# Routed expert outputs scattered to token rows, with GpSimd weighing half of them at the end of a decoder layer

## The chip, the cores and the metric

The kernel runs on one core of a Trainium2 chip. Five engines with queues of their own work on one on-chip memory: TensorE (PE, matrix products into the accumulator memory PSUM), VectorE (DVE), ScalarE (ACT), GpSimd (POOL) and SyncE (SP, which mostly issues DMAs). [...]The metric is device time in microseconds, a median over runs; the profile is one execution recorded by the hardware.

## What is computed

One post-norm decoder layer on 2048 tokens of 256 features (8 sequences of 256), in float32: self-attention with 16 heads, then three rounds of slot attention with a gated recurrent cell against a context of 120 rows, then a feed-forward stage, each followed by a layer norm. The change touches only the last stage:

```python
router_probs = softmax(x @ gate_w + gate_b)                   # 8 experts
expert_values, expert_indices = top_k(router_probs, k=2)
expert_values = expert_values / (sum(expert_values) + 1e-09)
h = gelu(einsum('bsd,edi->bsei', x, ew1) + eb1)
all_outputs = einsum('bsei,eid->bsed', h, ew2) + eb2
moe_out = einsum('bse,bsed->bsd', weights_E, all_outputs)      # the chosen two only
return layernorm(2 * x + mlp(x, sh_w1, sh_b1, sh_w2, sh_b2) + moe_out)
```

(The layer norm gets the residual sum once more, so x enters twice.) Each token needs two of the eight experts and, besides, one shared MLP with the same sizes (256 to 1024 to 256).

## The kernel before

Tokens lie in four blocks of 512 (`X[i]`, 128 partitions by 4 groups of 128 tokens by 256 features); `XT[i]` is the same block transposed, `Z[i]` the block's output sum.

**Routing.** When a block leaves the second stage, `route_rest` finds its two experts (`hot1`, `hot2`, weights `wt1`, `wt2`). `place(i)` gives each of the 1024 (token, choice) pairs a row in a table `xd` in DRAM, in which every expert owns 2048 rows, and scatters the tokens there: eight indirect DMAs from GpSimd's queue, 128 rows of 1 KB each (L909). Rows without a token stay zero, for which both `xd` and `yd` were filled with zeros earlier (L543), each 16640 rows.

**Tiles.** `tables` (L920) cuts the rows in use into 23 tiles, 16 of 256 rows and 7 of 128, each of one expert, whose number and first row are read from SBUF into registers of SyncE (`value_load`, L1130 and L1144). Per tile, `tile_fetch` loads its rows (`xg`), `tile_weights` and `tile_weights2` load the expert's two 1 MB matrices, `tile_turn` transposes the rows on TensorE and copies them out on VectorE (`xgT`), `tile_up` does the first product with GELU on ScalarE, `tile_down` the second, adds the bias on VectorE (`yo`), and stores it to the same rows of `yd` (L1180).

**Shared MLP.** It runs in eight units of 256 tokens: `shared_up(u)` and two halves of `shared_down(u)`. Units 0 to `SHARED_FIRST` - 1 = 3 stand before the tiles and cover the routing; units 4 to 7 stand after them.

**The end.** `fetch_back(i)` gathers the two outputs of each token from `yd` by the slots that `place` had computed (eight indirect DMAs of 128 rows on GpSimd's queue per block, L1190). `take_back(i)` adds them, weighted, to `Z[i]` in eight VectorE instructions (L1204). `finish` is the layer norm: statistics on VectorE (L221, L222), reciprocal root by Ln and Exp on ScalarE (L130, L131), three small refining steps (L236 to L238) and the scaling (L242) on VectorE, then the store.

**What sets the order.** TensorE and ScalarE follow the program everywhere. VectorE and GpSimd are ordered by a planner during the middle of the kernel, but from the last `tile_down` on all four follow the order in which the program is written. SyncE's queue is ordered by the planner. A DMA on SyncE's queue also waits for the DMA eight before it on the same semaphore.

Of the kernel before, what the change touches and what calls it, by code (L numbers as in the profile page):

```python
# [10 lines left out]
F32 = mybir.dt.float32  # L11
I32 = mybir.dt.int32
# [32 lines left out]

ROWS = NE * NT + RT

SHARED_FIRST = 4

NY = 16  # L50
LN_EPS = 1e-5
RMS_EPS = 1e-6
ATT_EPS = 1e-6
# [8 lines left out]
def decoder_kernel(  # L62
# [44 lines left out]
            nc.scalar.copy(dst, src)  # L107


    X = [act.tile([P, NSUB, D], F32, tag=f"X{i}", name=f"X{i}") for i in range(NBLK)]  # L110
    XT = [act.tile([P, DC, BLK], F32, tag=f"XT{i}", name=f"XT{i}") for i in range(NBLK)]

    def load_x(i):
# [36 lines left out]
    )  # L150


    xd = tc.dram_tile([ROWS, D], F32, name="xd")
    yd = tc.dram_tile([ROWS, D], F32, name="yd")


    for h in range(2):
# [378 lines left out]
    b2p = stage2.enter_context(tc.tile_pool(name="b2", bufs=2))  # L536

    shared = load_shared()
    zeros = b1.tile([P, D], F32, name="zeros")
    nc.gpsimd.memset(zeros, 0.0)  # L540

    for table in (xd, yd):
        nc.sync.dma_start(  # L543
            table.rearrange("(p r) d -> p r d", p=P), zeros.unsqueeze(1).to_broadcast([P, ROWS // P, D])
        )

    fh = ctx.enter_context(tc.tile_pool(name="fh", bufs=2, side="right"))

# [1 line left out]
    nsub_all = NBLK * NSUB  # L550
    hot1 = fr.tile([P, nsub_all, NE], F32, name="hot1")
    hot2 = fr.tile([P, nsub_all, NE], F32, name="hot2")
    wt1 = fr.tile([P, nsub_all], F32, name="wt1")
    wt2 = fr.tile([P, nsub_all], F32, name="wt2")
    slots = [fr.tile([P, nsub_all], I32, name=f"slot{j}") for j in range(2)]

    cur = fr.tile([P, nsub_all, NE], F32, name="cur")
# [272 lines left out]
    def route_rest(i):  # L830

        shape = [P, NSUB, NE]

        def t(name):
            return fr2.tile(shape, F32, tag=name, name=f"{name}_{i}")

        def s(name):
            return fr2.tile([P, NSUB], F32, tag=name, name=f"{name}_{i}")

        def wide(a):  # L840
            return a.unsqueeze(2).to_broadcast(shape)

        pl = bank(f"pl_{i}")[:, 0 : NSUB * NE].rearrange("p (n e) -> p n e", e=NE)
        for n in range(NSUB):
            for dc in range(DC):
                nc.tensor.matmul(
                    pl[:, n, :], XT[i][:, dc, ts(n, P)], gate_sb[:, dc, :], start=dc == 0, stop=dc == DC - 1
                )
        pb, mx, sm = t("pb"), s("mx"), s("sm")
        tt(pb, pl, gate_b.unsqueeze(1).to_broadcast(shape), ALU.add)  # L850
        nc.vector.tensor_reduce(mx, pb, AX.X, ALU.max)
        tt(pb, pb, wide(mx), ALU.subtract)
        nc.scalar.activation(pb, pb, AF.Exp)
        nc.vector.tensor_reduce(sm, pb, AX.X, ALU.add)
        nc.vector.reciprocal(sm, sm)
        tt(pb, pb, wide(sm), ALU.mult)
        rankb = rank.unsqueeze(1).to_broadcast(shape)

        def best(src, k, hot):
            top, first = s(f"top{k}"), s(f"first{k}")  # L860
            nc.vector.tensor_reduce(top, src, AX.X, ALU.max)
            tt(hot, src, wide(top), ALU.is_equal)
            tt(hot, hot, rankb, ALU.mult)
            nc.vector.tensor_reduce(first, hot, AX.X, ALU.max)
            tt(hot, hot, wide(first), ALU.is_equal)
            return top

        blk = ts(i, NSUB)
        top1 = best(pb, 1, hot1[:, blk, :])
        rest = t("rest")  # L870
        nc.vector.scalar_tensor_tensor(rest, hot1[:, blk, :], -2.0, pb, ALU.mult, ALU.add)
        top2 = best(rest, 2, hot2[:, blk, :])
        den = s("den")
        tt(den, top1, top2, ALU.add)
        nc.vector.tensor_scalar(den, den, TOPK_EPS, None, ALU.add)
        nc.vector.reciprocal(den, den)
        tt(wt1[:, blk], top1, den, ALU.mult)
        tt(wt2[:, blk], top2, den, ALU.mult)
        tt(cur[:, blk, :], hot1[:, blk, :], hot2[:, blk, :], ALU.add)
        for g in range(i * NSUB, (i + 1) * NSUB):  # L880
            tt(before[:, g + 1, :], before[:, g, :], cur[:, g, :], ALU.add)


    puts = []

    def place(i):

# [18 lines left out]
        for n in range(NSUB):  # L906
            for slot in slots:
                g = i * NSUB + n
                put = nc.gpsimd.indirect_dma_start(  # L909
                    out=xd[:, :],  # L910
                    out_offset=bass.IndirectOffsetOnAxis(ap=slot[:, g : g + 1], axis=0),
                    in_=X[i][:, n, :],
                    in_offset=None,
                )
                if puts:
                    tc.declare_no_dep(put.ins, group="puts", reason="other rows")
                tc.add_to_no_dep_group("puts", put.ins)
                puts.append(put)

    def tables():  # L920

# [77 lines left out]
        for a, b, n in ((te, te2, float(NE)), (tr, tr2, none)):  # L999
            nc.vector.scalar_tensor_tensor(b, b, -n, free, ALU.add, ALU.mult)  # L1000
            tt(a, a, b, ALU.add)
        nc.vector.tensor_scalar(te, te, float(NE - 1), None, ALU.min)
        tei = fr.tile([P, NTILE], I32, name="tei")
        nc.vector.tensor_copy(tei, te)
        tri = fr.tile([P, NTILE], I32, name="tri")
# [111 lines left out]
        tt(z, z, po, ALU.add)  # L1117
        yield

    TI = {}  # L1120

    def groups(t):
        return 2 if t < NPAIRT else 1
# [4 lines left out]
    def tile_fetch(t):  # L1128

        row = nc.sync.value_load(tri[0:1, t : t + 1], min_val=0, max_val=ROWS - RT)  # L1130
        xg = f2.tile([P, 2, D], F32, tag="xg", name=f"xg_{t}", bufs=4)[:, 0 : groups(t), :]
        load = nc.sync.dma_start(xg, rows_of(xd, row, t))
        for put in puts:
            tc.add_manual_dep(
                load.ins,
                put.ins.name,
                mybir.DependencyInfo(mybir.DependencyClass.Sync, mybir.DependencyReason.DATA),
                reason="rows of the table",
            )
        TI[t] = [row, xg]  # L1140

    def tile_weights(t):

# [4 lines left out]
        b2t = f2.tile([P, D], F32, tag="b2t", name=f"b2t_{t}", bufs=3)  # L1148
        nc.sync.dma_start(w1_sb, ew1[ds(e, 1), :, :].rearrange("e (c p) f -> p (e c) f", p=P))
        nc.sync.dma_start(bt, vecs[:, ds(e * FC, FC)])  # L1150
        TI[t] += [w1_sb, w2_sb, bt, b2t, e]

    def tile_weights2(t):

        row, xgT, w1_sb, w2_sb, bt, b2t, e = TI[t]
        nc.sync.dma_start(w2_sb, ew2[ds(e, 1), :, :].rearrange("e (c p) d -> p (e c) d", p=P))
        nc.sync.dma_start(b2t, b2[ds(e, 1), :].to_broadcast([P, D]))

    def tile_turn(t):
# [5 lines left out]
                nc.tensor.transpose(pt[:, dc, ts(k, P)], xg[:, k, ts(dc, P)], ident)  # L1165
        xgT = f2.tile([P, DC, RT], F32, tag="xgT", name=f"xgT_{t}")[:, :, 0 : n * P]
        nc.vector.tensor_copy(xgT, pt)  # L1167
        TI[t][1] = xgT

    def tile_up(t):  # L1170
        row, xgT, w1_sb, w2_sb, bt, b2t, e = TI[t]
        HT["t", t] = up(w1_sb, bt, xgT, f"t{t}")

    def tile_down(t):
        row, xgT, w1_sb, w2_sb, bt, b2t, e = TI.pop(t)
        n = groups(t)
        po = down(w2_sb, HT.pop(("t", t)), f"t{t}", groups=n)
        yo = f2.tile([P, 2, D], F32, tag="yo", name=f"yo_{t}")[:, 0:n, :]
        tt(yo, po[:, 0:n, :], b2t.unsqueeze(1).to_broadcast([P, n, D]), ALU.add)
        nc.sync.dma_start(rows_of(yd, row, t), yo)  # L1180

    Y = {}

    def fetch_back(i):

        for n in range(NSUB):
            for j, slot in enumerate(slots):
                g = i * NSUB + n
                y = f2.tile([P, D], F32, tag="y", name=f"y_{g}_{j}", bufs=NY)
                nc.gpsimd.indirect_dma_start(  # L1190
                    out=y,
                    out_offset=None,
                    in_=yd[:, :],
                    in_offset=bass.IndirectOffsetOnAxis(ap=slot[:, g : g + 1], axis=0),
                )
                Y[g, j] = y

    def take_back(i):

        for n in range(NSUB):  # L1200
            g = i * NSUB + n
            for j, wt in enumerate((wt1, wt2)):
                z = Z[i][:, n, :]
                nc.vector.scalar_tensor_tensor(z, Y.pop((g, j)), wt[:, g : g + 1], z, ALU.mult, ALU.add)  # L1204

    def finish(i, n0, n1):
        layernorm(Z[i][:, n0:n1, :])
# [11 lines left out]
    def parts(u):  # L1219
        next(part[u])  # L1220
        next(part[u])
# [11 lines left out]
    place(3)  # L1233
    next(part[1])
    tei, tri = tables()
    for t in TILES[:2]:
        tile_fetch(t)
    tile_weights(TILES[0])
    tile_weights2(TILES[0])
    for u in range(2, SHARED_FIRST):  # L1240
        shared_up(u)
        if u == SHARED_FIRST - 1:
            tile_fetch(TILES[2])
            tile_weights(TILES[1])
            tile_turn(TILES[0])
        parts(u)
    for u in range(SHARED_FIRST, nunit):
        shared_bias(u)
    for k, t in enumerate(TILES):
# [14 lines left out]
    engines = {mybir.EngineType.PE, mybir.EngineType.Activation, mybir.EngineType.DVE, mybir.EngineType.Pool}  # L1264
    ctx.enter_context(tc.manual_schedule(engines=engines))
    half = NSUB // 2
    shared_up(4)
    fetch_back(0)
    shared_up(5)
    fetch_back(1)  # L1270
    take_back(0)
    parts(4)
    take_back(1)
    shared_up(6)
    nc.scalar.preload_act_table_set(LNEXP)
    for i in range(2):
        finish(i, 0, NSUB)
    fetch_back(2)
    parts(5)
    shared_up(7)  # L1280
    nc.scalar.preload_act_table_set(LNEXP)  # L1281
    take_back(2)
    finish(2, 0, NSUB)
    fetch_back(3)
    next(part[6])
    take_back(3)
    next(part[6])
    finish(3, 0, half)
    po = [bank(f"pf_s7_{a}")[:, 0:D] for a in range(half)]
    hT = HT.pop(("s", 7))  # L1290
# [71 lines left out]
```

## Time and profile before

| | before |
|---|---|
| median of 3 runs | 1041.12 us (1041.05 to 1042.68) |
| the profiled execution | 1039.3 us |
| its span | 1037.6 us |
| TensorE busy | 1023.9 us (99%), at a granted clock of 0.999 |
| VectorE busy | 486.6 us (47%), 1378 instructions |
| ScalarE busy | 466.3 us (45%) |
| GpSimd busy | 264.1 us (25%), 280 instructions |
| zero fill of xd and of yd | 16640 KB each, landed 51.3 us and 99.4 us after their issue |
| indirect DMAs to xd (L909) and from yd (L1190) | 32 and 32, 8.39 MB in all |
| DMA traffic | 144.24 MB, 139 GB/s on average |

The span is the time between the first and the last recorded event; 1.7 us of the execution lie outside it. A group in the profile is named by source line, engine and operation, with what it writes and reads; a time in square brackets is idle time of the engine before an instruction and what ended it. TensorE's busy time counts pipelined products, so 99% says that it hardly ever waits, not that each product is as fast as can be.

### The profile page before, as it was taken

To read this page: it belongs to the slowest core of one execution; us is meant where nothing else is said; L and a number is where in the kernel's file an instruction comes from. 1 tells how busy PE (TensorE), PEld (TensorE's weight loads), DVE (VectorE), ACT (ScalarE), POOL (GpSimd) and SP (SyncE) were. 2 spreads that over 40 slices of the span, in tenths; PEclk is the share of its full clock that TensorE was granted. 3 is DMA by queue.
4 is the path that set the end of the run, shared out by engine and by line. 5 is a ranking of instruction groups with operands and counts; after the bars stand their busy time and mean duration, and the time that the engine had idled before them with its cause. 6 is when DMAs were issued, how large, how long until landed. Compare 5 with 4: busy or idle time off the path is not lost. (4 is left out here: it accounts for less than half of the span.)

```text
span 1037.6 us, 13707 instructions
## 1 busy us (share of the span) xinstructions
PE 1023.9 (99%) x4686; PEld 711.2 (69%) x4686; DVE 486.6 (47%) x1378; ACT 466.3 (45%) x1156; POOL 264.1 (25%) x280
## 2 busy tenths in 40 slices
PE   9999999999999999999999999999999999999997
PEld 5444555555546755556565567988888888888886
DVE  4778776877897542444444579600010101010157
ACT  3568776766685034455455434322222322222232
POOL 2333422633587221122212014410000000000172
PEclk9999999999999999999999999999999999999999
DMA  9844434434467399950000001166666676765143
GB/s 324 132 76 93 86 69 76 77 62 76 77 115 161 125 348 348 349 172 0 1 1 0 1 16 57 62 193 228 219 219 213 224 235 221 230 208 194 50 121 103
DMA packets 195492, 144.24 MB, mean 139 GB/s; under 512 B 107551, under 2 KB 185951, under 8 KB 195423
## 3 DMA queue, kind: packets, MB, share of 16 engines
q1 hardware_dynamic: 191263, 132.88, 45.5%
q0 software_dynamic: 3072, 8.39, 2.5%
q10 hardware_dynamic: 1088, 2.10, 0.5%
q8 instruction: 37, 0.61, 0.2%
q14 instruction: 32, 0.26, 0.1%
HBM read 72.70 MB, written 45.48 MB: 114 GB/s over the span
## 5 line engine op out<-in xcount | busy, mean ns | idle before, releaser
L1071 ACT ACTIVATE hT_t<-ph_t,bt 128x256 f32<-128x256 f32 (+1 forms) x184 | 71.3, 438 | 202.6 <-issue 139.1
L353 ACT ACTIVATE sc<-sc,nmax 128x128 f32<-128x128 f32 (+1 forms) x256 | 113.2, 443 | 86.0 <-DVE nmax L340 85.5
L368 POOL TENSOR_TENSOR sc<-sc,sums 128x256 f32<-128x256 f32 (+1 forms) x128 | 105.4, 845 | 162.8 <-DVE sums L365 162.0
L1062 PE MATMUL ph_t<-xgT,w 128*128 128x256 f32 (+1 forms) x736 | 140.3, 348 | 0.8 <-ACT hT_t L1071 0.8
L1076 PE MATMUL pf_t<-w,hT_t 128*128 128x256 f32 x624 | 138.3, 379 | 0.0
L1062 PEld LDWEIGHTS ph_t<-xgT,w 128*128 128x128 f32 x736 | 123.8, 190 | 15.0 <-ACT hT_t L1071 1.0
L756 PE MATMUL gate<-XT,whh_sb 128*128 128x512 f32 x288 | 133.8, 593 | 0.0
L1076 PEld LDWEIGHTS pf_t<-w,hT_t 128*128 128x128 f32 x624 | 116.9, 190 | 15.0
L1190 POOL DMA_INDIRECT y<-yd,slot x32 | 31.0, 969 | 308.2 <-PE ph_s L1062 298.7
L396 DVE COPY pT<-turned 128x1536 uint16<-128x1536 uint16 x64 | 89.8, 1403 | 1.2 <-DMA turned<-planes 1.2
L756 PEld LDWEIGHTS gate<-XT,whh_sb 128*128 128x128 f32 x288 | 54.2, 189 | 48.5 <-issue 46.2
L340 DVE CUSTOM_DVE_ANT_0 sc<-pp,mask 128x128 f32<-128x128 f32 (+1 forms) x256 | 75.8, 352 | 8.8 <-PE pp L328 8.2
L1167 DVE COPY xgT<-xg 128x512 f32<-128x512 f32 (+1 forms) x23 | 14.0, 610 | 131.7 <-PE xg L1165 131.7
L765 PEld LDWEIGHTS gate<-at,G 120*128 120x128 f32 x288 | 54.5, 189 | 29.9 <-issue 23.3
L613 DVE TENSOR_TENSOR yo<-pf_t,b2t 128x512 f32<-128x512 f32 (+1 forms) x23 | 14.0, 610 | 127.9 <-PE pf_t L1076 127.9
L384 ACT COPY planes<-sc 128x1536 uint16<-128x1536 uint16 x48 | 70.6, 1470 | 6.7 <-POOL sc L368 6.7
L765 PE MATMUL gate<-at,G 120*128 120x256 f32 x288 | 72.1, 379 | 0.4 <-DVE at L613 0.4
L303 PE MATMUL pq<-XT,wq_sb 128*128 128x512 f32 x128 | 63.4, 618 | 0.2 <-DVE XT L105 0.2
L303 PE MATMUL pq<-XT,wk_sb 128*128 128x512 f32 x128 | 63.2, 616 | 0.0
L313 PE MATMUL pv<-wv_sb,XT 128*128 128x512 f32 x128 | 59.7, 594 | 0.0
L410 PE MATMUL po<-pT,v 128*64 128x256 f32 (+1 forms) x512 | 55.7, 338 | 2.4 <-DVE pT L396 1.5
L426 PE MATMUL py<-wo_sb,ot 128*128 128x256 f32 x256 | 57.9, 381 | 0.0
(209 smaller groups left out, 1429.5 us busy)
## 6 DMA issues: line engine op xcount, KB each, us to landing
w<-in_ew_dram SPq DMA_DIRECT2D x46, 1024.0 KB, 5.5
xd<-zeros SPq DMA_DIRECT2D x1, 16640.0 KB, 51.3
yd<-zeros SPq DMA_DIRECT2D x1, 16640.0 KB, 99.4
xg<-xd SPq DMA_DIRECT2D x16, 256.0 KB, 5.2
yd<-yo SPq DMA_DIRECT2D x16, 256.0 KB, 5.6
b2t<-in_b_dram SPq DMA_DIRECT2D x23, 128.0 KB, 5.3
sh<-in_sh_w_dram SPq DMA_DIRECT2D x2, 1024.0 KB, 6.6
X<-in_x_dram SPq DMA_DIRECT2D x3, 512.0 KB, 11.6
```

Of the source, the lines that this page charges most:

```text
L303: nc.tensor.matmul(pq, w[:, dc, ts(pr, P)], XT[i][:, dc, :], start=dc == 0, stop=dc == DC - 1)
L313: nc.tensor.matmul(pv, XT[i][:, dc, ts(n, P)], wv_sb[:, dc, ts(hf, 512)], start=dc == 0, stop=dc == DC - 1)
L340: nc.vector.tensor_tensor_reduce(out=sc[:, h, seg[t]], in0=pp[h][:, seg[t]], in1=mask[:, seg[t]], scale=-(HD**-0.5), scalar=3.0e38, op0=AL ...
L353: nc.scalar.activation(sc[:, h, seg[t]], sc[:, h, seg[t]], AF.Exp, scale=-1.0, bias=nmax[:, t, h : h + 1], accum_out=sums[:, t, h : h + 1],)
L368: nc.gpsimd.tensor_tensor(sc[:, :, seg[t]], sc[:, :, seg[t]], sums[:, t, :].unsqueeze(2).to_broadcast([P, 2, w]), ALU.mult,)
L384: nc.scalar.copy(planes, words)
L396: nc.vector.tensor_copy(pT.rearrange("p h c -> p (h c)").bitcast(U16).rearrange("p (n w) -> p w n", w=2), turned.rearrange("p (w c) q -> p ...
L756: nc.tensor.matmul(pg[:, oc, :], whh_sb[:, dc, o], XT[i][:, dc, :], start=dc == 0, stop=not given and dc == DC - 1,)
L765: nc.tensor.matmul(pg[:, oc, ts(bi, S)], G[:, BPB * i + bi, o], AT_[p][:, bi, :], start=not hidden, stop=not hidden or bi == BPB - 1,)
L1062: nc.tensor.matmul(ph[:, a, 0:w], w1_sb[:, dc, ts(c, P)], rhs[:, dc, :], start=dc == 0, stop=dc == DC - 1,)
L1071: nc.scalar.activation(hT[:, c, 0:w], ph[:, a, 0:w], AF.Gelu_apprx_tanh, bias=bias[:, c : c + 1])
L1076: nc.tensor.matmul(po, hT[:, c, ts(a, P)], w2_sb[:, c, :], start=c == 0, stop=c == FC - 1)
```

## The change

- **Token rows carry their address.** `X[i]` becomes the first 256 columns of `XW[i]`, 272 columns wide. Column 256 holds 2 x (token + 1), column 257 the rank of the token's first expert, which `best` now writes there. The rows of `xd` are 272 wide too (1088 bytes).
- **Scatter instead of gather.** In `tile_turn`, three small VectorE instructions per tile work out the target row of each output: 2 x (token + 1), plus one if the tile's expert is the token's first choice, or an unused row where the table row was empty. `tile_down` writes its rows there with one indirect DMA per 128 rows on GpSimd's queue (39 in all) in place of the plain store on SyncE's. `yd` has 9090 rows and is no longer filled with zeros. `fetch_back` becomes one plain load of 1 MB per block on SyncE's queue, which waits for all 39 scatters; it lands in the expert weights' buffers, and all four are issued at once.
- **Token scatters in pairs.** In `place`, a small GpSimd memset stands after each pair of scatters. It writes a spare column of the groups just sent and to be sent next, and so waits until the pair has landed.
- **Weighing on GpSimd.** `take_back` of blocks 0 and 2 runs on GpSimd: one product of 2048 elements per partition and two sums of 1024. Blocks 1 and 3 stay on VectorE.
- **Order.** `SHARED_FIRST` is 5. The fetches of tiles 1 and 2 stand behind the weights of tile 0. `tile_turn` of the first tile stands after the last early unit instead of before its second half. The end is rearranged as below.

```diff
-SHARED_FIRST = 4
+SHARED_FIRST = 5
...
-    for table in (xd, yd):
-        nc.sync.dma_start(
-            table.rearrange("(p r) d -> p r d", p=P), zeros.unsqueeze(1).to_broadcast([P, ROWS // P, D])
-        )
+    nc.sync.dma_start(
+        xd.rearrange("(p r) d -> p r d", p=P), zeros.unsqueeze(1).to_broadcast([P, ROWS // P, DW])
+    )
...
+            if n + 1 < NSUB:
+                nc.gpsimd.memset(XW[i][:, n : n + 2, DW - 1 : DW], 0.0)
...
+        to = f2.tile([P, 2], I32, tag="to", name=f"to_{t}", bufs=6)
+        own, none = (f2.tile([P, 2], F32, tag=tag, name=f"{tag}_{t}")[:, 0:n] for tag in ("own", "none"))
+        g = 2 * t if n == 2 else NPAIRT + t
+        nc.vector.scalar_tensor_tensor(
+            own, xg[:, :, D + 1], tile_rank[:, t : t + 1], xg[:, :, D], ALU.is_equal, ALU.add
+        )
+        nc.vector.scalar_tensor_tensor(none, xg[:, :, D], 0.0, unused[:, g : g + n], ALU.is_equal, ALU.mult)
+        tt(to[:, 0:n], own, none, ALU.add)
...
-        nc.sync.dma_start(rows_of(yd, row, t), yo)
+        for k in range(n):
+            put = nc.gpsimd.indirect_dma_start(
+                out=yd[:, :],
+                out_offset=bass.IndirectOffsetOnAxis(ap=to[:, k : k + 1], axis=0),
+                in_=yo[:, k, :],
+                in_offset=None,
+            )
...
+        y = wff.tile([P, NSUB, 2, D], F32, tag=f"w{1 + i % 2}", name=f"y_{i}")
+        load = nc.sync.dma_start(
+            y, yd[2 * (i * BLK + 1) : 2 * ((i + 1) * BLK + 1), :].rearrange("(n p j) d -> p n j d", p=P, j=2)
+        )
+        after(load, outs)
...
+        if i % 2 == 0:
+            w = wt[:, ts(i, NSUB), :].unsqueeze(3).to_broadcast([P, NSUB, 2, D])
+            nc.gpsimd.tensor_tensor(y, y, w, ALU.mult)
+            for j in range(2):
+                nc.gpsimd.tensor_tensor(Z[i], Z[i], y[:, :, j, :], ALU.add)
+            return
...
-    for t in TILES[:2]:
-        tile_fetch(t)
+    tile_fetch(TILES[0])
     tile_weights(TILES[0])
     tile_weights2(TILES[0])
+    for t in TILES[1:3]:
+        tile_fetch(t)
     for u in range(2, SHARED_FIRST):
         shared_up(u)
-        if u == SHARED_FIRST - 1:
-            tile_fetch(TILES[2])
-            tile_weights(TILES[1])
-            tile_turn(TILES[0])
         parts(u)
+    tile_weights(TILES[1])
+    tile_turn(TILES[0])
...
-    shared_up(4)
-    fetch_back(0)
+    for i in range(NBLK):
+        fetch_back(i)
     shared_up(5)
-    fetch_back(1)
-    take_back(0)
-    parts(4)
-    take_back(1)
     shared_up(6)
     nc.scalar.preload_act_table_set(LNEXP)
-    for i in range(2):
-        finish(i, 0, NSUB)
-    fetch_back(2)
+    take_back(0)
+    take_back(1)
     parts(5)
+    finish(1, 0, NSUB)
+    finish(0, 0, NSUB)
+    take_back(2)
+    parts(6)
+    take_back(3)
     shared_up(7)
     nc.scalar.preload_act_table_set(LNEXP)
-    take_back(2)
     finish(2, 0, NSUB)
-    fetch_back(3)
-    next(part[6])
-    take_back(3)
-    next(part[6])
     finish(3, 0, half)
```

## The prediction

> **What bounds the kernel now.** First the chain that ended last, in order of time (start, length, engine, tile, line):
>
> ```profile
> 975.73 13.81 PE ph_s L1062 x64
> ...
> 1010.26 6.92 PE ph_s L1062 x32
> ...
> 1029.29 0.34 DVE Z L613
> ...
> 1034.08 0.41 DVE Z L242
> ```
>
> From 1.1 us to 1017 us it is TensorE without a break; after that ScalarE and VectorE. TensorE's timeline shows one of the few pauses, where a product follows at once on the transposes whose copy it needs, and the last products:
>
> ```profile
> 703.57 7.14 PE L1062 MATMUL ph_t<-xgT,w 128*128 128x256 f32 x32 [0.83 <-ACT hT_t L1071]
> ...
> 1017.01 13.98 PE L1076 MATMUL pf_s<-sh,hT_s 128*128 128x256 f32 x64
> ```
>
> The table by stages, for the last stretch (PE, PEld, DVE, ACT, POOL busy):
>
> ```profile
> 1031.00:1037.60 6.60, 0.00 (x0) 0.00 (x0) 2.62 (x11) 0.50 (x2) 0.00 (x0) 0.89 0.11 40
> ```
>
> So TensorE works to 1031.0 us, one add and one layer norm follow to 1034.5, one store and the closing to 1037.6. Between 1.1 and 1031.0 TensorE is idle for about 6 us in all. Its instructions are the same in number after the change. Hence there is little to win: VectorE takes the last product 0.9 us late (1031.81 against 1030.95), and a few waits of half a microsecond stand elsewhere. The question is what the change makes late.
>
> **The change part by part.**
>
> *Zero fill of yd, 16.6 MB less.* It runs from 355 us to 455 us, and TensorE's only pauses there are 0.45 and 0.52 us, behind VectorE. Nothing to win. The remaining fill is 6% bigger, ends about 410 us, and its first reader comes at 618 us.
>
> *Wider rows, iotas, the rank.* Four memsets and four iotas on GpSimd of 0.15 us each, by the iota rows, between its mask work (done at 2.1 us) and its next work at 12.9 us: hidden. The built program shows no wait of the x loads on them.
>
> *Token scatters in pairs.* Before, a scatter takes 1.26 us from one to the next and lands 2.4 us after its issue. The memset waits for the second of a pair: 1.26 + 2.4 + 0.6 for memset and semaphores = 4.3 us a pair instead of 2.5. Blocks 0 and 1 have 22 us each, so it is hidden. Blocks 2 and 3 are interleaved by the planner (pairs of one block run while the other's land); stepping through its order from 660.8 us I get the last landing at 686.6 us, against 682.3 before. The fetch of tile 0 waits for it; behind it on SyncE stand its weights, the fetches of tiles 1 to 3, and 40 register loads of 0.57 us each (27 such took 691.8 to 707.2 us before), 23 us, and then tile 2's weights, issued about 716.6. Meanwhile `SHARED_FIRST` moves the tiles 13.8 us later: tile 0 is wanted at 708.6 and tile 2's weights at 731.5, landing 5.5 us after issue. Covers of some 9 us each; cost nothing.
> VectorE's address steps for tiles 0 to 3 stand, in its queue, ahead of the copy that the first tile needs; the last waits for tile 3's rows, which land about 699 us. Same cover. Later address steps (0.16 us each) wait for rows that land some 6.6 us into a slot, where TensorE wants the copy at 10.8 us or later: nothing.
>
> *First transpose moved.* Its copy had 7 us of products above it; now the first tile's products follow at once. The quoted pause is the same case (transposes end at 702.58 in the chain, products start at 703.57): **+1.0 us** on TensorE.
>
> *Stores become scatters.* 39 at 1.26 us on an idle GpSimd over 280 us, 5.6 us a tile at most: hidden, except the last two. 32 gathers of 1.26 us go.
>
> *The end.* Let E be the end of the last tile: 975.73 + 13.81 + 1.0 = 990.5 us. TensorE's order then gives: units 5 and 6 up to E+13.8, their downs to E+20.7 and E+27.6, unit 7 up to E+34.5, its down to E+41.4. The scatters are issued to E+3 and land at E+4.6; four loads of 1 MB, 5.2 us for the first (weights of that size land in 5.5) and 3.2 each after it at the 324 GB/s of the first slice: E+9.9, 13.0, 16.3, 19.5.
> VectorE's queue is in program order: weigh block 1, add unit 5, finish 1, finish 0, add unit 6, weigh block 3, finish 2, finish 3. *Unhindered:* the add of unit 5 can't be before E+20.7. From the rows of before: add 0.7; finish 4.7 (moments 2.2, ScalarE 0.6, steps 0.6, scaling 1.3); finish 4.7; add 0.6; weighing 3.7; finish 4.7; half a finish 3.0; the last two groups 2.6 and 2.7. E+48.1 = 1038.6, against 1034.5: **+4.1 us**, of which 1.0 is the transpose. TensorE stops at E+41.4, so VectorE's chain, no longer TensorE, sets the end: behind the add of unit 5 stand 27 us of VectorE work beside 21 us of products.
>
> *GpSimd beside VectorE.* Before, no arithmetic on GpSimd stands in the tail. What it does to VectorE shows at the start of the second stage (start, length):
>
> ```profile
> 340.93 0.16 DVE L236 SCALAR_TENSOR_TENSOR step<-mv,rstd 128x4 f32<-128x4 f32 x1 [0.60 <-ACT rstd L131]
> ...
> 354.39 3.76 POOL L702 TENSOR_TENSOR sq<-XT 128x1024 f32<-128x1024 f32 x2
> ...
> 354.50 0.43 DVE L221 BATCH_NORM_STATS2 bnst<-X 128x6 f32<-128x256 f32 x1
> ...
> 356.35 1.82 DVE L237 SCALAR_TENSOR_TENSOR step<-step,rstd 128x4 f32<-128x4 f32 x1
> ...
> 358.11 2.49 POOL L703 TENSOR_TENSOR sq<-sq 128x512 f32<-128x512 f32 x2
> 358.20 1.19 DVE L238 SCALAR_TENSOR_TENSOR rstd<-step,rstd 128x4 f32<-128x4 f32 x1
> 359.43 2.28 DVE L242 TENSOR_SCALAR X<-X,mv,rstd 128x256 f32<-128x256 f32 x4
> ```
>
> A step of 0.16 us lasts until the GpSimd product ends at 358.15; the next until the next one ends; the first scaling too; the statistics pass untouched. One VectorE instruction gets through between two of GpSimd. The weighing instruction (128x256) isn't seen beside GpSimd arithmetic here. [...]
> GpSimd's lengths:
>
> ```profile
> L368 POOL TENSOR_TENSOR sc<-sc,sums 128x512 f32<-128x512 f32 x64 | 68.1, 1065 | 0.0
> L368 POOL TENSOR_TENSOR sc<-sc,sums 128x256 f32<-128x256 f32 x64 | 40.0, 625 | 162.8 <-DVE sums L365 162.0 <-DMA turned<-planes 0.8
> ```
>
> 1.72 ns per element and 0.185 us: the product of 2048, broadcast alike, takes 3.7 us; a sum of 1024, as the bias add of X at L421, 2.4. [...]
> From E+9.9 GpSimd runs product 0, two sums and product 2 (12.2 us), and VectorE's eight weighings of block 1 (3.8 us) go between and after: done at E+25.8, not before E+20.7. Add of unit 5: E+26.4, where it was E+21.4. Then block 2's two sums run to E+31.1, over finish 1, whose steps were due at E+29.2: +1.9. Together **+6.9 us**; GpSimd is then done. If only the steps were held, not the weighing: +1.9.
> ScalarE's GELU of unit 7 stands behind finish 0 and now stalls unit 7 on TensorE by 7 us, but it ends 0.7 us before finish 2 asks for ScalarE: hidden.
>
> **Sum.** 1.0 + 3.1 + 6.9 = +11.0 us on the span of 1037.6, so 1048.6, and with 1.7 us around it 1050.3 for the profiled execution. The median shown is 1.8 us above that execution (1041.12 to 1039.3); on it, **1052.1 us**, 1.06% slower.
>
> **Rivals.** (1) The lock hardly holds the weighing: 1041.12 + 4.1 = 1045.3, to 1048.5 with part of it. For it: no row shows this form held. Against: the same operation held for 1.8 us. Chance 0.15. (2) The front of the tiles stalls as well: the pairs land over 9 us later than I stepped, or rows arrive late behind VectorE's address steps; each microsecond beyond goes straight onto TensorE. 5 to 10 us more, 1057 to 1062. For it: 40 register loads and four waits in VectorE's queue that were not there; against: the covers counted above. 0.12. (3) No loss: VectorE's chain keeps ahead of TensorE, since 16 weighings (7.5 us) leave it. It must have done with the first half of finish 3 by E+41.4; then the end is TensorE's, 1031.0 + 1.0 + 2.7 = 1034.7 us for 1034.5 before: 1041.3 us. But even unhindered that half is done only at E+42.8, and a whole last group more follows. 0.06. (4) Faster by more than the 0.2% (2 us) that can be told from no change: the scatter ends the gathers' waits (12.6 us on VectorE before), but these lay beside products; 2 us would have to come out of TensorE's 6 us of pauses, some 1038. 0.03.
>
> **The numbers.** Forecast 0.64, in 1048.5 to 1055.5. The range 1045.0 to 1057.5 adds most of rival 1 and the longer product, and leaves some 0.2 out. Faster 0.03, within 0.2% 0.06, slower 0.91.
>
> **What would show it.** Profile of after: a pause of some 0.8 us before the first ph_t; none elsewhere before E; weighings and one step of finish 1 well over 0.5 us while GpSimd sums; TensorE idle near unit 7's up; some 7 us between the last product and VectorE's end. Wrong if the weighings keep 0.48 us beside GpSimd, or if TensorE waits for xgT or w in the tiles.

## The result, and the profile after

The changed kernel takes 1055.24 us (median of 4 runs, 1053.7 to 1055.96), the kernel before 1041.9 us on the same chip: a ratio of 1.0132, 95% interval 1.0118 to 1.0147. The forecast was 1052.1 us. Slower was right. The time lies 3.1 us above the forecast and only 0.3 us below the upper end of the inner range (1055.5).

The profiled execution took 1053.7 us with a span of 1051.9, 14.3 us more than the 1037.6 before; forecast were 11.0. TensorE is busy for 1028.4 us (1023.9 before) at a mean granted clock of 0.992 (0.999). First the view of what TensorE waited for: total, times, longest.

```profile
PE ph_s L1098 <- ACT hT_s L1107: 6.4, 1, 6.4
...
PE ph_t L1098 <- DVE xgT L1197: 0.9, 1, 0.9
```

These are the only two waits that the profile before doesn't have: the first turn, which stands bare now, and the up product of unit 7, which waits for ScalarE. Neither is 14 us. Next the timeline of TensorE around the end of the routing and at the end of the tiles (start, length, engine, line, names, shapes, count). A count is one of records: the profile has two for every float32 product.

```profile
648.42 3.64 PE L857 MATMUL pl<-gate_sb,XT 128*128 128x8 f32 x32
651.91 8.84 PE L1098 MATMUL ph_s<-XT,sh 128*128 128x256 f32 x32
...
711.60 7.17 PE L1098 MATMUL ph_t<-xgT,w 128*128 128x256 f32 x32 [0.95 <-DVE xgT L1197]
...
992.09 13.98 PE L1098 MATMUL ph_s<-XT,sh 128*128 128x256 f32 x64
```

The second line is 32 records of 256 columns. The profile before has for them:

```profile
652.15 7.15 PE L1062 MATMUL ph_s<-XT,sh 128*128 128x256 f32 x32
```

The last line begins unit 5, and so gives E, the end of the last tile: 992.09, where the forecast had 990.5. Then the end of the kernel, from the timeline of all engines:

```profile
1003.04 3.60 POOL L1251 TENSOR_TENSOR y<-y,wt 128x2048 f32<-128x2048 f32 x1 [7.55 <-DMA y<-yd]
...
1005.50 11.97 DVE L1259 SCALAR_TENSOR_TENSOR Z<-y,wt,Z 128x256 f32<-128x256 f32 x8 [12.52 <-DMA y<-yd]
...
1006.72 4.90 POOL L1253 TENSOR_TENSOR Z<-Z,y 128x1024 f32<-128x1024 f32 x2
...
1011.58 3.78 POOL L1251 TENSOR_TENSOR y<-y,wt 128x2048 f32<-128x2048 f32 x1
1017.39 0.68 DVE L624 TENSOR_TENSOR Z<-Z,pf_s 128x512 f32<-128x512 f32 x1
...
1018.21 4.78 POOL L1253 TENSOR_TENSOR Z<-Z,y 128x1024 f32<-128x1024 f32 x2 [2.85 <-DVE Z L624]
...
1019.72 3.62 PE L1098 MATMUL ph_s<-XT,sh 128*128 128x256 f32 x16
...
1020.80 2.20 DVE L247 SCALAR_TENSOR_TENSOR step<-mv,rstd 128x4 f32<-128x4 f32 x1 [0.60 <-ACT rstd L132]
...
1029.73 6.41 PE L1098 MATMUL ph_s<-XT,sh 128*128 128x256 f32 x16 [6.39 <-ACT hT_s L1107]
...
1037.03 1.28 ACT L1335 ACT_TABLE_LOAD   x1
1038.33 0.30 ACT L131 ACTIVATE rstd<-mv,eps_ln 128x4 f32<-128x4 f32 x1
...
1038.89 0.16 DVE L247 SCALAR_TENSOR_TENSOR step<-mv,rstd 128x4 f32<-128x4 f32 x1 [2.85 <-ACT rstd L132]
...
1048.65 0.41 DVE L253 TENSOR_SCALAR Z<-Z,mv,rstd 128x256 f32<-128x256 f32 x1
```

The eight weighings of block 1 take 12.0 us, while GpSimd multiplies and adds; a step of finish 1 takes 2.2. For the first 16 records of unit 7 TensorE needs 3.62 us, for the 16 after its pause 6.41. VectorE waits 2.85 us for ScalarE in finish 2, where 0.6 is usual, and ends at 1049.06, that is E+57.0 (forecast E+55.0). The clock stands in the table by stages (length, then PE, PEld, DVE, ACT and POOL busy, then the granted clock):

```profile
653.00:656.30 3.30, 3.30 (x10) 2.59 (x9) 3.30 (x34) 2.12 (x3) 1.93 (x2) 0.50 0.21 80
...
1020.00:1022.00 2.00, 2.00 (x11) 1.77 (x10) 1.38 (x2) 0.50 (x2) 1.92 (x2) 1.00 0.00 0
1028.00:1030.00 2.00, 0.27 (x1) 0.28 (x2) 1.96 (x6) 1.99 (x5) 0.00 (x0) 0.59 0.01 4
1030.00:1032.00 2.00, 2.00 (x5) 1.58 (x6) 1.89 (x6) 0.40 (x2) 0.00 (x0) 0.50 0.72 254
...
1036.00:1038.00 2.00, 2.00 (x11) 1.77 (x10) 0.05 (x1) 1.81 (x3) 0.00 (x0) 1.00 0.00 0
```

TensorE ran at half clock behind the pause. The entries "2.00 (x5)" and "2.00 (x11)" say the same: five records in the time of eleven. It also did so from 653.0 to 656.3 us, without a pause before it.

### The profile page after: what moved, and what is told of

Its sections match the earlier page's. It is cut to its first block, busy times and chain, and to the rows that moved or that the text cites. A ratio compares the mean times of both kernels' runs of the same rounds, so it can differ in the third digit from the quotient of the medians.

```text
span 1051.9 us, 13713 instructions
## 1 busy us (share of the span) xinstructions
PE 1028.4 (98%) x4686; PEld 714.0 (68%) x4686; DVE 498.4 (47%) x1432; ACT 466.0 (44%) x1156; POOL 289.1 (27%) x314
## 3 DMA queue, kind: packets, MB, share of 16 engines
q10 hardware_dynamic: 1088, 2.10, 0.5%
## 5 line engine op out<-in xcount | busy, mean ns | idle before, releaser
L1223 POOL DMA_INDIRECT yd<-yo,to x39 | 37.4, 958 | 271.5 <-DVE yo L624 266.6
L1098 PE MATMUL ph_s<-XT,sh 128*128 128x256 f32 x256 | 61.5, 401 | 6.4 <-ACT hT_s L1107 6.4
L1202 DVE SCALAR_TENSOR_TENSOR own<-xg,tile_rank 128x2 f32<-128x2 f32 (+1 forms) x23 | 5.1, 220 | 120.0 <-DMA xg<-xd 120.0
L1098 PEld LDWEIGHTS ph_s<-XT,sh 128*128 128x128 f32 x256 | 51.4, 202 | 14.9 <-ACT hT_s L1107 7.2
```

The source lines that it names most:

```text
L1098: nc.tensor.matmul(ph[:, a, 0:w], w1_sb[:, dc, ts(c, P)], rhs[:, dc, :], start=dc == 0, stop=dc == DC - 1,)
```

## The experiments

Twelve runs were made, on four chips. On two of them the kernel before took 1041.4 and 1042.5 us, as in the result; on the two others 1073.8 and 1073.0. I call these chips of the first and of the second kind. Times are set against the kernel before on the same chip only. Between chips I compare the traces by two points: E, and how long after E VectorE ends, the tail. The tail of the changed kernel is 57.0 us on both kinds, so that I compare it between all runs that keep its end. One of them, e3_turn, has the same end and a tail of 56.0, so a single tail is good to a microsecond. The tail of the kernel before is not the same on both kinds.

| kernel | kind | E | tail | median | ratio to before |
|---|---|---|---|---|---|
| before (first profile) | first | 975.6 | 58.9 | 1041.9 | |
| changed (first profile) | first | 992.1 | 57.0 | 1055.2 | 1.0132 (1.0118 to 1.0147) |
| e1_vector | second | 1000.6 | 52.0 | 1055.4 | 0.9825 (0.9793 to 0.9858) |
| e2_unweighed | second | 995.0 | 48.3 | 1049.4 | 0.9787 (0.9753 to 0.9822) |
| e3_turn | second | 999.3 | 56.0 | 1060.5 | 0.9883 (0.9856 to 0.9911) |
| e4_filler | second | 1002.0 | 58.9 | 1063.9 | 0.9899 (0.9870 to 0.9928) |
| c_before | second | 990.4 | 75.4 | 1070.6 (one) | |
| c_after | second | 1000.5 | 57.0 | 1059.2 | 0.9878 (0.9846 to 0.9910) |
| e5_filler13 | second | 999.2 | 54.7 | 1057.6 | 0.9862 (0.9828 to 0.9896) |
| e6_first4 | second | 988.0 | 58.1 | 1049.5 | 0.9782 (0.9749 to 0.9816) |
| e7_serial | first | 996.6 | 57.0 | 1059.6 | 1.0183 (1.0159 to 1.0206) |
| e8_nopairs | first | 992.1 | 57.0 | 1053.6 | 1.0113 (1.0095 to 1.0131) |
| e9_onegap | first | 982.6 | 58.1 | 1045.3 | 1.0033 (1.0018 to 1.0047) |
| e10_late | first | 976.4 | 58.1 | 1041.1 | 0.9995 (0.9987 to 1.0003) |

The theory at the start was that of the prediction, with one addition from the trace: VectorE's chain is too long for three units of products (some 3 us), GpSimd's arithmetic holds VectorE (some 6 to 7), the half clock after TensorE's pause delays ScalarE (2.2). Rivals: the weighings are slow because the loads of `y` land beside them; the clock falls for another reason.

### All weighing on VectorE, and no weighing of two blocks

```diff
-        if i % 2 == 0:
+        if False:
```

> All four blocks are weighed on VectorE, none on GpSimd; all else as in the changed kernel. E is the end of the last tile (992.1 us there), and VectorE's end stood at E+57.0. If GpSimd's arithmetic holds VectorE instruction by instruction: VectorE gets 16 more weighings (7.7 us) and loses 10.2 us of holding; its chain is then weigh 0 and 1 from E+11.0 to E+18.7, add of unit 5 at E+20.9, end at about E+52.5, so 4.5 us less: span 1047.4, median about 1050.7. If the long weighings had another cause (the loads of y landing beside them), the work moved onto VectorE is added: 7.7 us more, median about 1063.

```diff
-    take_back(0)
...
-    take_back(2)
```

> Blocks 0 and 2 are not weighed at all (their routed outputs are left out of the result); VectorE's own instructions are the same as in the changed kernel. If GpSimd's arithmetic holds VectorE: the weighings of block 1 fall from 12.0 to 3.8 us, the held step of finish 1 from 2.2 to 0.16 us, VectorE's end goes to the unhindered E+48.1, or E+49 with a rest of ScalarE's delay: span about 1043.5, median about 1046.8. If the loads that land at the same time slow VectorE: weighings stay long, median 1054 to 1055.

Their medians can't be set against the expected ones, which were worked out for the first kind of chip. The tails can. Groups by line and form between 1003 and 1024 us in the changed kernel, and in the same part of the end of e2_unweighed, 1006 to 1026 us (busy, mean ns | idle before):

```profile
L1259 DVE SCALAR_TENSOR_TENSOR Z<-y,wt,Z 128x256 f32<-128x256 f32 x8 | 11.8, 1508 | 12.7 <-DMA y<-yd 12.5
...
L232 DVE BATCH_NORM_STATS2 bnst<-Z 128x6 f32<-128x256 f32 x4 | 1.6, 400 | 0.0
```

```profile
L1259 DVE SCALAR_TENSOR_TENSOR Z<-y,wt,Z 128x256 f32<-128x256 f32 x8 | 3.6, 483 | 12.6 <-DMA y<-yd 12.5
L232 DVE BATCH_NORM_STATS2 bnst<-Z 128x6 f32<-128x256 f32 x8 | 3.2, 401 | 0.0
```

Without GpSimd's arithmetic, and with the same four loads of `y`, a weighing takes 483 ns instead of 1508; the statistics, one operand, take 400 ns either way. The loads are not the cause. The tail falls to 48.3 us, where the prediction had 48.1 for the unhindered chain. With all 32 weighings on VectorE the tail is 52.0 us (expected 52.5): VectorE doing twice the weighing is 5 us faster than VectorE with GpSimd's help. Some 2.3 of these 5 us are the half clock (below), since e1_vector has no pause of TensorE in its tail.

### The first turn earlier

```diff
         shared_up(u)
+        if u == SHARED_FIRST - 1:
+            tile_turn(TILES[0])
         parts(u)
...
-    tile_turn(TILES[0])
```

> The turn of the first tile stands before the last early unit's second half again. Theory: the pause of 0.95 us before the first product of the tiles goes, E comes 1.0 us earlier, and as the whole end hangs on E, the median is 1.0 us lower (1054.2). Rival: the pause only moves (the transposes find their rows late, or the gelu of the last early unit is then late): 1055.2.

The wait of 0.95 us for `xgT` is gone from the trace, and the first product follows at once. E is 1.2 us earlier than in c_after, of which 0.95 is this. The median, 1060.5, doesn't show a microsecond against c_after's 1059.2 from another chip. The wait is shown to go; its worth in the median is not.

### Something for TensorE to do in its pause

The filler stands between the two halves of unit 7's first product:

```diff
         for c2 in range(FC // 2):
+            if c2 == 2:
+                between()
...
-    shared_up(7)
+    po = [bank(f"pf_s7_{a}")[:, 0:D] for a in range(half)]
+
+    def filler():
+        for _ in range(26):
+            nc.tensor.matmul(po[0], shared[0][:, 0, 0:P], XT[3][:, 0, 0:D], start=True, stop=True)
+
+    shared_up(7, filler)
```

> 26 products of 256 columns, into a bank that is overwritten afterwards, stand in TensorE's queue at the place of its 6.4 us pause in unit 7 (5.7 us of them at full clock). Theory: the half clock after the pause comes from the pause; with the filler the 16 products after it take 3.6 us instead of 6.4, the gelu of unit 7 ends about 2.5 us earlier, finish 2 gets ScalarE in time, and VectorE ends about 2.2 us earlier: median 1053.0. Rival: the clock falls there for another reason: it falls with the filler too, median 1055.2 or more.

A size in this expectation was wrong: a float32 product of 256 columns stands in the trace as two records of 0.22 us, so 26 of them took 11.39 us, overran the pause and made the tail longer (58.9); the 16 records behind them took 3.62 us. e5_filler13 has half as many:

> As the filler before, with half as many products: 13, since one of 256 columns in float32 takes 0.22 us twice, so 5.7 us at full clock. Theory: the pause of 6.4 us and the half clock after it go, the 16 products behind take 3.6 us, the gelu of unit 7 ends about 2.5 us earlier, VectorE's wait for ScalarE in finish 2 shrinks from 2.85 to 0.6 us: end at E+54.7 instead of E+57.0, 2.2 us less than the changed kernel on the same chip. Rival: the clock falls during the filler too: E+57 or later.

TensorE in e5_filler13, from the timeline (the first line is the filler):

```profile
1030.32 5.78 PE L1340 MATMUL pf_s<-XT,sh 128*128 128x256 f32 x26
...
1036.83 3.72 PE L1100 MATMUL ph_s<-XT,sh 128*128 128x256 f32 x16 [0.73 <-ACT hT_s L1109]
```

The 16 records behind the filler now take 3.72 us instead of 6.41, VectorE's wait in finish 2 is 0.60, and the tail is 54.69 us: 2.28 less, as expected. Five traces have the pause (the changed kernel on both kinds, e3_turn, e7_serial, e8_nopairs; 6.34 to 6.49 us). The 16 records behind it take 5.31 us in e3_turn and 6.33 to 6.53 in the others, VectorE's wait in finish 2 is each time 3.57 us less (1.74 to 2.96), and the tails are 56.0 to 57.0. So the half clock came from the pause, and VectorE's wait from the half clock. Useless products shortened the tail, because they kept the clock (granted 1.00 from 1028 to 1040 us, where the changed kernel has 0.50 from 1030 to 1034); the median, 1.5 us below c_after's on the same chip, is not clear of the noise.

### The kernel before and after on a chip of the second kind

> The kernel before, for its profile on this chip: a span near 1037.6 us where the chip is like the first one; near 1072 us where it is like the second, and then with pauses of TensorE of some 32 us in all that the first profile doesn't have. Theory: they stand where instructions arrive late, as the 2.5 to 6.0 us pauses at 678 us of the last four runs did. Rival: a lower clock alone (a mean of 0.984 for 0.999 is worth 16 us at most).

> The changed kernel as it is, beside the kernel before on the same chip, since on the chip of the last four runs the kernel before took 1073.8 us where it had taken 1041 to 1043 on another. If the change costs what it cost there on any chip: 1.0118 to 1.0147 times the kernel before. If the kernel before loses time on that chip in something that the change removed, the ratio is near 0.98 to 0.99.

There the change is faster: 0.9878. The kernel before loses 14.9 us ahead of E and 16.4 us in its tail against its first profile; the changed kernel loses 8.4 us ahead of E (4.6 of them in one wait of TensorE on "issue") and nothing in its tail. In c_before's tail GpSimd issues a gather every 1.25 us from 994 to 1024 us, and the timeline of TensorE reads:

```profile
1021.05 0.59 PE L1062 MATMUL ph_s<-XT,sh 128*128 128x256 f32 x1 [1.51 <-issue]
1023.15 0.59 PE L1062 MATMUL ph_s<-XT,sh 128*128 128x256 f32 x1 [1.51 <-issue]
1025.24 0.58 PE L1062 MATMUL ph_s<-XT,sh 128*128 128x256 f32 x1 [1.51 <-issue]
1026.64 7.90 PE L1062 MATMUL ph_s<-XT,sh 128*128 128x256 f32 x24 [0.82 <-issue]
```

"issue" means that the engine waited for nothing that the profile shows. Single records come 2.1 us apart until soon after the gathers stop (the twenty-fourth of 32 is issued at 1023.2, the next at 1029.6), then 24 run on. The first such wait begins at 1011 us; TensorE ran on through the first 17 us of gathers. Beside the token scatters ScalarE does the same (from c_before's timeline, during its 16 scatters from 666 to 686 us):

```profile
675.85 0.84 ACT L1071 ACTIVATE hT_s<-ph_s,vec_sb 128x256 f32<-128x256 f32 x2 [10.52 <-issue]
683.65 0.84 ACT L1071 ACTIVATE hT_s<-ph_s,vec_sb 128x256 f32<-128x256 f32 x2 [6.96 <-issue]
```

In the first profile the first of these two waits is 8.9 us, for TensorE's products, and the second 0.9; the same indirect DMAs follow each other there at the same 1.25 to 1.27 us, and the list of what TensorE waited for has not one "issue". So the change removes 16.4 us in the tail there (no gathers) and 6.4 ahead of E, and its own cost stays. That the waits coincide with trains of indirect DMAs is shown; why, and what makes a chip of either kind, is not.

The theory of the expectations was that instructions arrive late, a supposition that no trace of this case shows. The traces speak against it. They list DMAs of instructions as queues of their own; the first line is the larger of the two in c_before's whole span, as in the first profile, and the other two are all that c_before lists from 1003 to 1045 us:

```profile
q8 instruction: 37, 0.61, 0.2%
...
q0 software_dynamic: 1252, 3.41, 28.9%
q1 hardware_dynamic: 528, 0.52, 3.5%
```

No instructions landed in these 42 us, nor from 668.5 to 697 us, where ScalarE's waits end, so no recorded DMA of instructions ended the waits. The record itself differs between the kinds: the view of DMAs gives the landing of indirect ones in all six profiles of the first kind and in none of the eight of the second (before, then c_before):

```profile
xd<-X,slot POOLq DMA_INDIRECT x32, 2.4
...
xd<-X,slot POOLq DMA_INDIRECT x32
```

Most of their landings are missing there (270 records in c_before's trace, 1023 in the first), so "issue" can stand for a wait whose record is lost, and that recording itself slows such a chip is a rival that no run here excludes.

Two kernels were to test the theory, by more room between the scatters and by none; they ran on a chip of the first kind.

```diff
+            if i == 2 and n + 1 == NSUB:
+                nc.gpsimd.memset(XW[2][:, :, DW - 1 : DW], 0.0)
+                nc.gpsimd.tensor_copy(XW[3][:, :, DW - 1 : DW], XW[2][:, :, DW - 1 : DW])
```

> The changed kernel with one more dependence: the token scatters of block 3 start when those of block 2 have landed, so that every pair of them is followed by a gap of some 2 us (in the changed kernel pairs of the two blocks alternate and 14 of the 16 follow each other at 1.3 us, with two memsets that wait). On a chip like that of the last eight runs (kernel before 1073 us): theory: ScalarE and TensorE get their next instructions late while indirect DMAs follow each other without a gap; then the pause of 4.6 us at 680 us goes, and the half clock behind it, and the first product of the tiles stands at 712 to 714 us instead of 720.0; median 1052 to 1054 instead of 1059. The last scatter lands some 12 us later, at about 700 us, still before the first turn. Rival: the pause has another cause at that place (the tables, the register loads): it stays, 1059. On a chip like the first (kernel before 1041 us): no change against the changed kernel, 1054 to 1056.

```diff
-            if n + 1 < NSUB:
-                nc.gpsimd.memset(XW[i][:, n : n + 2, DW - 1 : DW], 0.0)
```

> The changed kernel without the memsets behind the pairs of token scatters: 16 scatters follow each other at 1.27 us, as in the kernel before. On the chip with the kernel before at 1073 us: theory of late instructions: the front loses as much as it does there in the kernel before, that is 14.9 us against the first chip, instead of 8.4: first product of the tiles at about 726 us, median about 1065. Rival (the pairs do nothing): 1059. On a chip like the first: 1054 to 1056, as the scatters are hidden there either way.

For the second kind both say nothing. On the first kind e8_nopairs has E at 992.1 and the first product at 711.60, as the changed kernel: the pairs cost nothing there. e7_serial was slower than expected there, 1.0183 against the 1.0132 of the result, and shows where the cover ends. VectorE in its timeline:

```profile
711.86 0.22 DVE L1205 SCALAR_TENSOR_TENSOR own<-xg,tile_rank 128x2 f32<-128x2 f32 x1 [2.65 <-DMA xg<-xd]
...
712.86 0.69 DVE L1200 COPY xgT<-xg 128x512 f32<-128x512 f32 x1
```

The address step of tile 3 waits for its rows, and the copy for tile 0, whose transposes were done at 708.9, stands behind it in VectorE's queue. TensorE waits 4.71 us, and the first of the products after it run at half clock (9.72 us for 32 records that take 7.17 in the changed kernel).

### Towards a better version

e6_first4 has four early units again, all weighing on VectorE, the turn of e3_turn, and an end ordered like that of the kernel before:

```diff
-SHARED_FIRST = 5
+SHARED_FIRST = 4
...
-    tile_fetch(TILES[0])
     tile_weights(TILES[0])
     tile_weights2(TILES[0])
-    for t in TILES[1:3]:
+    tile_weights(TILES[1])
+    for t in TILES[:3]:
         tile_fetch(t)
...
+    shared_up(4)
     shared_up(5)
+    take_back(0)
+    take_back(1)
+    parts(4)
     shared_up(6)
     nc.scalar.preload_act_table_set(LNEXP)
-    take_back(0)
-    take_back(1)
+    take_back(2)
+    finish(0, 0, NSUB)
+    finish(1, 0, NSUB)
     parts(5)
-    finish(1, 0, NSUB)
-    finish(0, 0, NSUB)
-    take_back(2)
-    parts(6)
-    take_back(3)
     shared_up(7)
     nc.scalar.preload_act_table_set(LNEXP)
+    take_back(3)
     finish(2, 0, NSUB)
+    parts(6)
     finish(3, 0, half)
```

> The scatter kept, with four early units again (four stay for the end), the weights of tiles 0 and 1 issued ahead of the first fetch, the first turn before the last early unit's second half, all weighing on VectorE, finishes 0 and 1 ahead of the add of unit 5. Theory: VectorE then has 14 us more of products beside its chain, TensorE sets the end again, E is 13.8 + 1.0 us earlier and the end is E+58.8 as before: a span of 1037 to 1039 us on a chip like the first, that is 12 to 14 us less than the changed kernel and within 2 us of the kernel before. Rival: the front stalls (rows or weights of the first tiles late without the fifth unit): 4 to 8 us of that are lost, at the first tiles.

On the second kind: a tail of 58.1 us with 13.8 us more of products in it, no pause of TensorE in the tail, and 0.9782 of the kernel before, in spite of one wait of 6.2 us at 680 us (2.5 to 6.0 in the other runs of this kind). The next one drops the pairs of blocks 2 and 3 for one gap between the blocks (the edit of e7_serial, with the memset of pairs only for `i < 2`):

> The version with four early units, and the scatters of blocks 2 and 3 without pairs but with one gap of some 3 us between the blocks. Theory: the gap lets the late instructions in before the pause at 678 us; the pause of 6.2 us and its half clock shrink, 3 to 8 us less than the 1049.5 us of that version where the kernel before takes 1073 us. Rival: one gap comes too early or is too short: 1049 or more. On a chip like the first: 1039 to 1041, no slower than the kernel before.

It ran on the first kind: 1045.3 us, a ratio of 1.0033, 4 us above the upper end of what was expected there. TensorE waited 3.28 us for the first rows. Three weights of 1 MB had been issued from 677.7 us on, and from 680 to 690 us the DMAs moved 367 GB/s; that this delayed the last scatters is likely, but was not tested alone. The last version puts the first fetch in front again, keeps the pairs, turns after the last early unit, and ties the address steps to the bias add in `tile_down`:

```diff
+        out = nc.vector.tensor_tensor(yo, po[:, 0:n, :], b2t.unsqueeze(1).to_broadcast([P, n, D]), ALU.add)
...
+        first = nc.vector.scalar_tensor_tensor(
+            own, xg[:, :, D + 1], tile_rank[:, t : t + 1], xg[:, :, D], ALU.is_equal, ALU.add
+        )
+        after(first, [out])
+        second = nc.vector.scalar_tensor_tensor(none, xg[:, :, D], 0.0, unused[:, g : g + n], ALU.is_equal, ALU.mult)
+        after(second, [out])
```

> The version with four early units and all weighing on VectorE, with the token scatters in pairs again, the first fetch ahead of the weights (in the one-gap run the three weights of 1 MB landed beside the last scatters and the first rows came 3.3 us late), the first turn after the last early unit, and VectorE's three address steps of a tile behind its bias add instead of beside its turn, so that the copy of a first tile no longer waits in VectorE's queue for the rows of a later one. Theory: no pause before the first product of the tiles but the 0.95 us of the copy, first product at 698 to 699 us where the kernel before takes 1041 us (695.2 there), tail E+58.1, span 1038 to 1040, ratio 0.998 to 1.002; where the kernel before takes 1073 us, 1046 to 1050 and a ratio of 0.975 to 0.98. Rival: the front lacks the fifth unit all the same (weights of tile 2 behind the register loads): 3 to 8 us more, with TensorE waiting for w.

TensorE in e10_late's timeline:

```profile
694.40 0.60 PE L1195 MATMUL xg<-ident,xg 128*128 128x128 f32 x4
695.94 7.17 PE L1098 MATMUL ph_t<-xgT,w 128*128 128x256 f32 x32 [0.94 <-DVE xgT L1197]
```

E is 976.4, the tail 58.1, the span 1037.3 us, the ratio 0.9995 (0.9987 to 1.0003): the scatter costs nothing there in this form, and the 13 us that the change had lost on this kind are back. It doesn't beat the kernel before on this kind. On the second kind it was not run; e6_first4, with the same end, was 2.2% faster than the kernel before there and 0.9% faster than the changed kernel (1049.5 and 1059.2, same chip).

## Why the prediction was right, and where it was short

**What bounds the kernel; zero fill, iotas, gathers.** Right. Between 340 and 456 us TensorE is busy for 115.03 us, 115.04 before. Nothing was won on this kind of chip.

**Front.** Right. The first pair of block 2, with its memset, took 4.54 us (4.3). The first fetch is issued at 688.3 us, tile 3's address step stands at 703.3 (estimated 699), tile 2's weights are issued at 718.8 (716.6). The covers held. In e7_serial the first fetch is issued 8.8 us later (697.1), which used them up, and it paid as the second rival said, by rows that arrive late ahead of a copy in VectorE's queue.

**First transpose, +1.0.** 0.95. But E came at 992.09, not 990.5. The rest is 1.69 us at 652.9 to 656.3, where TensorE ran at half clock while busy, straight after 32 records of eight columns (the 8.84 us above). The prediction has no such term. It isn't a fixed price of the change: e7_serial and e10_late have 7.15 us there, e8_nopairs and e9_onegap have 8.84, and the kernel before, with the same products, 7.15 on the first kind and 8.83 on the second. I count it as chance. The times of single runs would fit it: the four of the kernel before in the result are 1041.1, 1041.1, 1042.7 and 1042.8 us, and the 14 of e10_late stand near 1039.2, 1041.0 and 1042.7. But one run of each kernel was traced, so that these steps are this loss isn't shown.

**The end, unhindered, +3.1.** The chain was estimated to end at E+48.1; e2_unweighed ends at E+48.3. Against the old tail less one unit (58.9 - 13.8 = 45.1) that is 3.2 us.

**GpSimd beside VectorE, +6.9.** 6.35: e5_filler13's tail less e2_unweighed's (54.69 - 48.34). Block 1 was weighed at E+25.4 (forecast E+25.8). That this came out is in part luck: the load of `y` landed 1.05 us later than forecast, and only four of the eight weighings were added to GpSimd's time (1.91 us behind it), the other four got through beside it. The held step cost 2.04 (1.9), the products took 3.60 and 3.78 us (3.7), the sums 2.4 (2.4). That GpSimd holds a weighing was the author's estimate, carried over from the steps, which are the same operation; no row of before shows this form held. The runs do: 1508 against 483 ns. The hold is the "lock" of the first rival. No run shows the 1.6 us of a longer product that the range counts: the two took 7.38 us together, 7.4 by the rows.

**The step that failed** is the last sentence of that part: unit 7 stalls by 7 us, "but it ends 0.7 us before finish 2 asks for ScalarE: hidden". The stall was 6.39 us. What the sum left out is what a stall does to TensorE: the clock was halved for the 16 records after it, 6.41 us instead of 3.62. These 2.8 us used up the cover (0.46 us of idle ScalarE in e5_filler13, forecast 0.7) and left 2.25 us, which VectorE waited in finish 2 and which e5_filler13 took away.

How long a stall it takes shows in e2_unweighed and e9_onegap, behind waits of 2.51 and 3.28 us (the granted clock is the third number from the end):

```profile
680.90:683.00 2.10, 2.08 (x10) 1.84 (x11) 0.00 (x0) 0.33 (x1) 1.21 (x2) 1.00 0.19 70
...
694.00:695.00 1.00, 1.00 (x4) 0.81 (x4) 0.77 (x3) 0.00 (x0) 0.00 (x0) 0.50 0.67 207
```

The first wait cost nothing more, the second another 1.8 us; behind the 4.71 us of e7_serial 2.55 us were lost, behind the five pauses of 6.34 to 6.49 us 1.69 to 2.91. In the list of what TensorE waited for before, the longest wait is 1.1 us, so that profile doesn't show what follows a stall of 7 us. That it would stay hidden was the author's estimate; the least of the losses behind the five pauses, 1.69 us, is more than the 0.7 us of cover.

Sum: 1.6 late at E, 2.0 in the tail, less 0.3 in the closing: 3.3 us, which with 11.0 is the 14.3 measured. The rivals: GpSimd did hold the weighing (not the first), the front didn't stall on this kind (not the second), and VectorE didn't keep ahead (not the third). That the change could be faster was given 0.03, on the ground that TensorE had 6 us of pauses in all; on the second kind of chip it had 16.5 us of "issue" waits alone, and it is faster. The profile of one chip could not show that.

## What to carry to other kernels

Moving work to an idle engine helps only if the two engines don't hold each other. Here a weighing took 1508 ns on average beside GpSimd's arithmetic and 483 without it, a step of the layer norm 2.20 us instead of 0.16, the statistics 0.40 us either way: take from a trace which forms are held, count those of the busy engine that stand beside the other's, and let one of them through between two of the other's (the first four weighings each ended 0.27 or 0.28 us after one of GpSimd's instructions). Price every stall of TensorE of some 3 us or more twice, as the stall and as the products behind it at half clock (3.28 us cost 1.8 more, 4.71 us 2.55). Take a queue's waits for DMAs from the slowest arrival in it: a small instruction for a later tile, placed early, can hold the copy that the present tile needs (TensorE waited 4.71 us in e7_serial). And look at the kernel on more than one chip before a change is judged by 1%: this one took 1.0132 of the time before on one kind and 0.9878 on the other.

## What the runs showed of the hardware that was not expected

- Two kinds of chip: the kernel before took 1041 to 1043 us on some and 1073 us on others, from one program; in the profile of the latter TensorE and ScalarE have waits on "issue" beside trains of indirect DMAs (on TensorE nine, 16.5 us in all, 5.8 at the longest). The cause is open; no DMA of instructions was recorded in these waits of TensorE.
- TensorE's clock was halved for 3.4 us in the midst of busy time, after 3.6 us of eight-column products (granted clock 0.50 from 653.0 to 656.3 us in the changed kernel); it cost 1.69 us and comes and goes between runs of kernels with the same products.
- A wait of TensorE of 3.28 us was followed by half clock, one of 2.51 us was not.
- A float32 product of 256 columns appears as two records of 0.22 us, 0.44 us in all.
